# Selective scan with four states per partition group, its sums as 0/1 products one step later, and the gelu calls of a block kept together

## The chip, the cores and the metric

The kernel runs on one core of a Trainium2 chip. The core has five engines with a queue each, worked through in order: TensorE (PE, matrix products; its weight loads are listed apart as PEld), VectorE (DVE), ScalarE (ACT), GpSimd (POOL) and SyncE (SP, which here only issues transfers, DMAs). The time is the device time of one execution in microseconds (us). Of the kernel before, ten executions are known, and one more that the hardware profiler recorded.

## The reference, cut to what matters

The kernel computes four layers of a small sequence model on 8 sequences of 256 positions with 128 channels. The change touches two of its steps. One is the state space step of layer 1 (256 inner channels, 16 states):

```
x_ssm = xc @ W_xproj
delta_raw = x_ssm[..., :1]
Bm = x_ssm[..., 1:1 + D_STATE]
Cm = x_ssm[..., 1 + D_STATE:]
delta = softplus(delta_raw * w_dt + b_dt)
A = -exp(A_log)
dA = exp(delta[..., None] * A)
dBx = delta[..., None] * Bm[:, :, None, :] * xc[..., None]
h = dA_t * h + dBx_t                       # for each position t
y = einsum('bdn,bn->bd', h, c_t)
y = (y + xc * D_param) * silu(z)
```

The other is the feed-forward part of the local attention of layer 0, run twice for each sequence: `a, g = split(h @ w1 + b1)`, then `h = a * gelu(g)`, with 341 channels in `a` and in `g`.

## The kernel before

The kernel is a row of stages. The change lies in the stage `local_mamba` (function `local_mamba`, L818), which works on the 8 sequences one by one. Each sequence first goes through two layers of `local_block` (L666: local attention and the gated feed-forward, called "local work" below), and its result `x_local` goes to `mamba_sequence` (L713), the state space step. `interleave` (L249) weaves these generators into one program: up to four sequences in local work, up to two in the state space step. Each `yield` gives the weight after which that generator's turn comes again. The program order made so is a priority. A planner that models durations then fixes, when the kernel is built, the order in which each engine gets its instructions. On the chip every engine takes them in that order and waits on semaphores where an input is late. `issue_after` (L396) adds an order without a wait, `wait_for` (L406) a wait. A tile of a pool has a tag and a number of buffers (`bufs`); a new tile of that tag has to wait until the oldest is released.

In `mamba_sequence` the 256 inner channels lie as two groups of 128 on the partitions (index `c`). POOL works out `d` (delta) and `u` (delta times xc) in L770 to L774; DVE does it for the last sequence. The 33 rows of `x_ssm` are written to DRAM (L746) and read back, each row spread over all 128 partitions, by `rows` (L748): two DMAs of 256 KB for every pair of states, three buffers. The loop over 8 steps `m` (L778) takes two states for all 256 channels at a time. A step is four Exp on ACT (L785, 128 partitions by 255) into one of three tiles `da`, then three DVE instructions over 1024 columns: `u` times B (L787), the scan (L789), times C (L790), and last two products on PE with the identity (L792, 128 by 512 columns, fp32). These add the step to `yp`, one PSUM bank with a column for each position of each of the two channel groups. After the loop DVE reads `yp` in L796.

In `local_block`, three products `g` (L691, two of 128 output channels and one of 85) are followed by three Gelu on ACT (L693). Gelu and Silu need other function tables than Exp and Ln, so a table load stands at each change; `exp_ln` (L414) asks for the Exp and Ln table again after the last of the three.

At the end of the stage, `beside` (L904) runs next to the last sequence: weights for the next stages are loaded by SP, folded on PE, and the routing of the next layer starts (`route1`).

Of the kernel before, what the change touches and what calls it, by code (L numbers as in the profile page):

```python
# [21 lines left out]
P = 128  # L22
B = 8
S = 256
# [53 lines left out]
def _tables():  # L78
    f = np.float32
    cols, n = [], 0  # L80
# [45 lines left out]
    add("iota8", np.tile(np.arange(8, dtype=f) - 8, (P, 1)))  # L126
    _C["n"] = n
# [27 lines left out]
def _layout(d):  # L155
# [3 lines left out]
    out = {}  # L159
# [25 lines left out]
    put("alog", d["L1_attn_A_log"].reshape(2, P, 16).transpose(0, 2, 1))  # L185
# [111 lines left out]
class _Kernel:  # L297
    def __init__(self, ctx, tc, ins, out):
# [33 lines left out]
        r = slice(_C["iota32"][0], _C["n"])  # L332
        self.rt = const.tile([P, r.stop - r.start], F32, name="route_tables")
# [59 lines left out]
    def mm(self, out, lhsT, rhs, start=True, stop=True):  # L393
        return self.nc.tensor.matmul(out, lhsT, rhs, start=start, stop=stop)  # L394
# [271 lines left out]
    def local_block(self, l, x, w, rot, work, local, small, pools):  # L666
# [23 lines left out]
        for c in range(3):  # L690
            self.mm(part(c), w1[:, 341 + c * P : 341 + c * P + size(c)], h2)  # L691
        for c in range(3):
            last = nc.scalar.activation(ge[0 : size(c), c, :], part(c), AF.Gelu, bias=self.v(f"b1g{l}", c)[0 : size(c), :])  # L693
# [19 lines left out]
    def mamba_sequence(self, b, x, y, na, das, work, scan):  # L713
# [29 lines left out]
        xs = work.tile([33, S], F32, tag="xs", name="xs", bufs=2)  # L743
# [4 lines left out]
        def rows(m):  # L748

            bc = scan.tile([P, 2, 2, S], F32, tag="bc", name="bc", bufs=3)  # L750
            for k in range(2):
                r = 1 + 16 * k + 2 * m
                src = xd[r : r + 2, :].rearrange("n s -> (n s)").unsqueeze(0).to_broadcast([P, 2 * S])
                nc.sync.dma_start(bc[:, k].rearrange("p n s -> p (n s)"), src)
            return bc

# [4 lines left out]
        e, r, d, t = tile("e"), tile("r"), tile("d", 2), tile("t")  # L761
# [11 lines left out]
        u = tile("u", 2)  # L773
        eng.tensor_mul(u, d, xc)  # L774
        yield 3.0
        yp = self.psum("Y", "y")
        shp = [P, 2, 2, S]
        for m in range(8):  # L778
            bc = rows(m)
            bn, cn = (bc[:, k].unsqueeze(2).to_broadcast(shp) for k in range(2))  # L780
            da = das[m % len(das)]
            for n in range(2):
                for c in range(2):
                    i = 16 * c + 2 * m + n
                    nc.scalar.activation(da[:, n, c, 1:S], d[:, c, 1:S], AF.Exp, scale=na[:, i : i + 1])  # L785
            hs = scan.tile(shp, F32, tag="hs", name="hs", bufs=3)
            nc.vector.tensor_tensor(hs, u.unsqueeze(1).to_broadcast(shp), bn, ALU.mult)  # L787
            line = lambda a: a.rearrange("p n c s -> p (n c s)")
            nc.vector.tensor_tensor_scan(line(hs), line(da), line(hs), 0.0, ALU.mult, ALU.add)  # L789
            nc.vector.tensor_tensor(hs, hs, cn, ALU.mult)  # L790
            for n in range(2):
                self.mm(yp, self.ident, flat(hs[:, n]), m == 0 and n == 0, m == 7 and n == 1)  # L792
            yield 2.3
        yg = tile("t")
        for c in range(2):
            nc.vector.scalar_tensor_tensor(yg[:, c, :], xc[:, c, :], self.v("dpar", c), yp[:, c * S : (c + 1) * S], ALU.mult, ALU.add)  # L796
# [21 lines left out]
    def local_mamba(self):  # L818
        nc, tc = self.nc, self.tc
        w = self.w0  # L820
        with (
# [20 lines left out]
            for i in range(3):  # L842
                d = one.tile([P, 2, 2, S], F32, name=f"da{i}")
                nc.gpsimd.memset(d[:, :, :, 0:1], 0.0)
                das.append(d)
# [17 lines left out]
            tiles.append(scan.tile([P, 4, S], F32, tag="bc", name="rg", bufs=3))  # L863
# [949 lines left out]
```

## Time and profile before

| what | value |
|---|---|
| median of 10 executions | 1848.66 us (1846.89 to 1854.51) |
| profiled execution, its own time | 1847.66 us |
| its span, first to last instruction | 1845.9 us |
| mean granted TensorE clock | 0.927 |
| busy over the whole span | PE 84%, DVE 59%, ACT 56%, POOL 31% |
| stage `local_mamba` | about 40 us to 925 us after the start |
| scans of the eight sequences | 280 us to 903 us |

The page's busy shares are means over stages with different limits, so the stage is read from stretches of the span. The waits name who ended an engine's idle time. The chain of waits is followed back from the last instruction and says whose work stood in the way at each moment.

### The profile page before, as it was taken

How to read it: one execution, taken by the hardware profiler on the slowest of the kernel's cores; microseconds unless marked ns; L12 is line 12 of the kernel's file. 1: busy time of each engine (PE TensorE's matmuls, PEld its weight loads, DVE VectorE, ACT ScalarE, POOL GpSimd, SP SyncE). 2: the span in 40 equal slices, each digit the busy share in tenths (PEclk: the TensorE clock that was granted, in tenths of full speed). 3: DMA queues.
4: the chain of work that ended last, by engine and by line, in shares of the span. 5: the costliest groups of instructions: out<-in, count | busy, mean ns of one | idle time of the engine just before them, and what ended most of it. 6: DMA issues, size and time to landing. Idle time of an engine off the chain costs nothing.

```text
span 1845.9 us, 28438 instructions
## 1 busy us (share of the span) xinstructions
PE 1556.3 (84%) x10810; PEld 940.1 (51%) x10810; DVE 1095.5 (59%) x2016; ACT 1027.8 (56%) x2704; POOL 563.6 (31%) x493
## 2 busy tenths in 40 slices
PE   3677887878787867678669999999997999899997
PEld 2244553544454444344256766666663654465554
DVE  5725457777777776868724445557444223567664
ACT  4557777776777785556225454455443223465654
POOL 1314443433443323210421111110112025354552
PEclk7789998989999988887779999999998999899998
DMA  4000012010202111246440000000101311000000
GB/s 177 1 1 1 1 36 57 26 53 20 76 17 71 51 45 49 57 149 195 125 120 9 4 10 7 7 5 2 40 3 31 83 48 30 1 4 7 4 4 10
DMA packets 58329, 75.51 MB, mean 41 GB/s; under 512 B 5868, under 2 KB 35236, under 8 KB 57168
## 3 DMA queue, kind: packets, MB, share of 16 engines
q1 hardware_dynamic: 52864, 67.57, 12.9%
q0 software_dynamic: 3216, 5.07, 1.0%
q8 instruction: 85, 1.39, 0.3%
q10 hardware_dynamic: 2112, 1.05, 0.2%
q14 instruction: 52, 0.43, 0.1%
HBM read 65.46 MB, written 9.71 MB: 41 GB/s over the span
## 4 chain that ended last, share of the span: by engine, by line
PE 53%; DVE 19%; ACT 12%; issue 7%; POOL 6%; DMA 2%; POOLq 0%; DVEq 0%; SPq 0%; ACTq 0%
PE vps L394 7%; PE sc L394 7%; PE kps L394 6%; DVE hs L789 4%; PE out L394 4%; PE pt L475 4%; PE o L394 3%; PE pu L394 3%; ACT e L647 3%; PE pg L394 3%; DVE hs L790 3%; DVE hs L787 2%; PE acc L394 2%; PE y L394 2%; PE hps L394 2%
## 5 line engine op out<-in xcount | busy, mean ns | idle before, releaser
L394 PE MATMUL y<-hs,ident 128*128 128x512 f32 x256 | 143.9, 690 | 43.6 <-DVE hs L790 43.6
L789 DVE TENSOR_TENSOR_SCAN hs<-da,hs 128x1024 f32<-128x1024 f32 x64 | 148.7, 2332 | 4.0 <-ACT da L785 3.5
L475 PE MATMUL pt<-ident,e 128*128 128x128 f32 x768 | 123.7, 287 | 29.6 <-POOL e L652 19.8
L1682 ACT ACTIVATE e<-sc,nm 128x128 f32<-128x128 f32 (+1 forms) x256 | 104.1, 424 | 60.4 <-DVE nm L1677 60.0
L652 POOL TENSOR_TENSOR e<-e,rc 128x1024 f32<-128x1024 f32 x32 | 72.1, 2253 | 201.2 <-DVE rc L651 201.1
L785 ACT ACTIVATE da<-d,na 128x255 f32<-128x255 f32 x256 | 112.1, 502 | 34.9 <-DVE hs L789 17.4
L1685 POOL TENSOR_TENSOR e<-e,rc 128x1024 f32<-128x1024 f32 x48 | 91.9, 1915 | 127.7 <-DVE rc L1684 94.6
L647 ACT ACTIVATE e<-sc,nm,rn 128x128 f32<-128x128 f32 x256 | 113.4, 465 | 25.2 <-DVE nm L642 25.0
L475 PEld LDWEIGHTS pt<-ident,e 128*128 128x128 f32 x768 | 89.4, 145 | 72.3 <-POOL e L652 26.4
L599 POOL TENSOR_TENSOR t<-t,t 128x512 f32<-128x512 f32 x64 | 89.0, 1390 | 95.4 <-DVE t L586 86.4
L1294 POOL TENSOR_TENSOR e<-e,rc 128x512 f32<-128x512 f32 x32 | 33.6, 1051 | 273.2 <-DVE rc L1293 160.4
L787 DVE TENSOR_TENSOR hs<-u,bc 128x1024 f32<-128x1024 f32 x64 | 86.6, 1362 | 41.8 <-POOL u L774 26.5
L394 PEld LDWEIGHTS y<-hs,ident 128*128 128x128 f32 x256 | 50.3, 212 | 96.8 <-DVE hs L790 55.8
L1269 ACT COPY kp<-kps 128x512 f32<-128x512 f32 x128 | 74.8, 584 | 40.7 <-PE kps L394 40.2
L477 ACT COPY ptsb<-pt 128x512 f32<-128x512 f32 x89 | 52.2, 587 | 80.3 <-PE pt L475 78.5
L1118 POOL DMA_INDIRECT got<-ybuf,get x48 | 45.6, 950 | 154.2 <-DMA ybuf<-ys 113.2
L477 DVE COPY ptsb<-pt 128x512 f32<-128x512 f32 x103 | 69.1, 685 | 32.0 <-PE pt L475 31.6
L394 PE MATMUL qk<-w_local,h 128*128 128x512 f32 x128 | 72.6, 655 | 17.8 <-DVE t L586 13.0
L790 DVE TENSOR_TENSOR hs<-hs,bc 128x1024 f32<-128x1024 f32 x64 | 82.0, 1289 | 0.2
L1677 DVE TENSOR_REDUCE nm<-sc 128x4 f32<-128x1024 f32 (+1 forms) x48 | 58.6, 1221 | 25.4 <-PE sc L394 25.1
L394 PE MATMUL sc<-km,q 64*128 64x512 f32 x192 | 70.5, 655 | 1.7 <-DVE FunctionType.Silu _12235 L1500 0.9
L1242 DVE BATCH_NORM_STATS2 st<-out 128x6 f32<-128x128 f32 x80 | 20.0, 288 | 81.0 <-PE out L394 74.0
(394 smaller groups left out, 3845.4 us busy)
## 6 DMA issues: line engine op xcount, KB each, us to landing
bc<-xs SPq DMA_DIRECT2D x128, 256.0 KB, 4.5
w_attn<-in_w_dram SPq DMA_DIRECT2D x4, 1024.0 KB
w_local<-in_w_dram SPq DMA_DIRECT2D x2, 1557.0 KB
places<-zeros SPq DMA_DIRECT2D x2, 1280.0 KB
w_moe<-in_e1gate_dram SPq DMA_DIRECT2D x8, 256.0 KB
w_moe<-in_e1up_dram SPq DMA_DIRECT2D x8, 256.0 KB, 7.7
w_moe<-in_e1down_dram SPq DMA_DIRECT2D x8, 256.0 KB, 5.4
w_moe<-in_e2rg_dram SPq DMA_DIRECT2D x8, 256.0 KB
```

Of the source, the lines that this page charges most:

```text
L394: return self.nc.tensor.matmul(out, lhsT, rhs, start=start, stop=stop)
L475: self.last = self.nc.tensor.transpose(pt[:, j * P : (j + 1) * P], src[:, j * P : (j + 1) * P], self.ident)
L477: self.nc.any.tensor_copy(sb.rearrange("p a b -> p (a b)"), pt)
L599: nc.gpsimd.tensor_add(t1, t1, t2)
L647: nc.scalar.activation(e[:, j, g, :], scs[:, j, g, :], AF.Exp, bias=nm[:, j, g : g + 1], scale=rq[:, j, g : g + 1], accum_out=sm[:, j, g : ...
L785: nc.scalar.activation(da[:, n, c, 1:S], d[:, c, 1:S], AF.Exp, scale=na[:, i : i + 1])
L787: nc.vector.tensor_tensor(hs, u.unsqueeze(1).to_broadcast(shp), bn, ALU.mult)
L789: nc.vector.tensor_tensor_scan(line(hs), line(da), line(hs), 0.0, ALU.mult, ALU.add)
L790: nc.vector.tensor_tensor(hs, hs, cn, ALU.mult)
L1269: nc.scalar.copy(k[:, 2 * i : 2 * i + 2, :].rearrange("p a b -> p (a b)"), ps)
L1682: nc.scalar.activation(e[:, i, :], sc[:, i, :], AF.Exp, bias=nm[:, i : i + 1], accum_out=sm[:, i : i + 1])
L1685: nc.gpsimd.tensor_tensor(e, e, rc.unsqueeze(2).to_broadcast([P, n, keys]), ALU.mult)
```

## The change

There are two parts.

**State space step.** A step now takes four states of 32 channels on the 128 partitions (partition 32n + h is state n of channel h) and four such groups of 32 channels along the columns, so the eight steps are two channel halves `c` by four sets `m` of four states. DVE and ACT run the same number of instructions of the same size. What feeds them changes: `d` and `u` are written to DRAM (`put`), and for each half `c` read back four times, once for each quarter of the partitions (`copies`, four DMAs for `d` and four for `u`; `d` has one buffer, `u` two). The second half is fetched after the first product of step 3. B and C of all 16 states come in one tile `bc` with one buffer, by four DMAs at the start of the sequence. The sum over the four states is a product with a 0/1 table `sum4` of 128 by 32: four products of 32 output channels by 256 columns for each step, each on its own quarter of the PSUM partitions. The sums of a step are put into the program one step later and ordered behind the PE instruction that was last put into the program before them. The scan steps of a sequence begin in the program only when those of the sequence before are all in it (`self.scanned`). `xs` has one buffer in place of two, `d` one, `u` takes over the buffer of `r`, and a step yields 2.5 in place of 2.3.

**Gelu.** The three Gelu of a block get high priority in the planner, and the first of them waits for the third product `g`.

```diff
+    add("sum4", i % 32 == np.arange(32)[None])
...
-    put("alog", d["L1_attn_A_log"].reshape(2, P, 16).transpose(0, 2, 1))
+    put("alog", d["L1_attn_A_log"].reshape(8, 32, 4, 4).transpose(2, 0, 3, 1))
...
-            self.mm(part(c), w1[:, 341 + c * P : 341 + c * P + size(c)], h2)
-        for c in range(3):
-            last = nc.scalar.activation(ge[0 : size(c), c, :], part(c), AF.Gelu, bias=self.v(f"b1g{l}", c)[0 : size(c), :])
+            m = self.mm(part(c), w1[:, 341 + c * P : 341 + c * P + size(c)], h2)
+        with self.tc.high_priority():
+            for c in range(3):
+                last = nc.scalar.activation(ge[0 : size(c), c, :], part(c), AF.Gelu, bias=self.v(f"b1g{l}", c)[0 : size(c), :])
+                if c == 0:
+                    self.wait_for(last, m)
...
-        def rows(m):
-            bc = scan.tile([P, 2, 2, S], F32, tag="bc", name="bc", bufs=3)
-            for k in range(2):
-                r = 1 + 16 * k + 2 * m
-                src = xd[r : r + 2, :].rearrange("n s -> (n s)").unsqueeze(0).to_broadcast([P, 2 * S])
-                nc.sync.dma_start(bc[:, k].rearrange("p n s -> p (n s)"), src)
-            return bc
+        bc = scan.tile([P, 2, 4, S], F32, tag="bc", name="bc", bufs=1)
+        for n in range(4):
+            src = bass.AP(tensor=xd.tensor, offset=xd.offset + (1 + n) * S, ap=[[0, 32], [4 * S, 8], [1, S]])
+            nc.sync.dma_start(bc[32 * n : 32 * n + 32].rearrange("p k m s -> p (k m) s"), src)
...
+        dram = [self.dram.tile([2 * P, S], F32, name=f"{n}{b}") for n in "du"]
+        def put(k, a):
+            nc.sync.dma_start(dram[k].rearrange("(c p) s -> p c s", c=2), a)
+        def copies(k, c):
+            a = scan.tile([P, 4, S], F32, tag="du"[k], name="du"[k], bufs=1 + k)
+            for n in range(4):
+                nc.sync.dma_start(a[32 * n : 32 * n + 32], dram[k][c * P : (c + 1) * P, :].rearrange("(g h) s -> h g s", h=32))
+            return a
...
-        u = tile("u", 2)
+        put(0, d)
+        u = tile("r")
         eng.tensor_mul(u, d, xc)
+        put(1, u)
+        dr, ur = copies(0, 0), copies(1, 0)
         yield 3.0
+        while self.scanned < b:
+            yield 0.5
         yp = self.psum("Y", "y")
-        shp = [P, 2, 2, S]
-        for m in range(8):
-            bc = rows(m)
-            bn, cn = (bc[:, k].unsqueeze(2).to_broadcast(shp) for k in range(2))
-            da = das[m % len(das)]
-            for n in range(2):
-                for c in range(2):
-                    i = 16 * c + 2 * m + n
-                    nc.scalar.activation(da[:, n, c, 1:S], d[:, c, 1:S], AF.Exp, scale=na[:, i : i + 1])
+        summed = deque()
+        def add(i, hs, last):
+            c, m = i // 4, i % 4
+            for g in range(4):
+                j = self.mm(yp[32 * g : 32 * g + 32, c * S : (c + 1) * S], self.c("sum4"), hs[:, g, :], m == 0, m == 3)
+                self.issue_after([j], last)
+        shp = [P, 4, S]
+        for i in range(8):
+            c, m = i // 4, i % 4
+            da = das[i % len(das)]
+            for g in range(4):
+                nc.scalar.activation(da[:, g, 1:S], dr[:, g, 1:S], AF.Exp, scale=na[:, 8 * m + 4 * c + g : 8 * m + 4 * c + g + 1])
             hs = scan.tile(shp, F32, tag="hs", name="hs", bufs=3)
-            nc.vector.tensor_tensor(hs, u.unsqueeze(1).to_broadcast(shp), bn, ALU.mult)
+            nc.vector.tensor_tensor(hs, ur, bc[:, 0, m, :].unsqueeze(1).to_broadcast(shp), ALU.mult)
+            if i == 3:
+                dr, ur = copies(0, 1), copies(1, 1)
             nc.vector.tensor_tensor_scan(line(hs), line(da), line(hs), 0.0, ALU.mult, ALU.add)
-            nc.vector.tensor_tensor(hs, hs, cn, ALU.mult)
-            for n in range(2):
-                self.mm(yp, self.ident, flat(hs[:, n]), m == 0 and n == 0, m == 7 and n == 1)
-            yield 2.3
+            nc.vector.tensor_tensor(hs, hs, bc[:, 1, m, :].unsqueeze(1).to_broadcast(shp), ALU.mult)
+            summed.append((i, hs))
+            last = self.pe_last
+            if i:
+                add(*summed.popleft(), last)
+            yield 2.5
+        add(*summed.popleft(), self.pe_last)
+        self.scanned = b + 1
```

More of the change, by code (lines that the diff above doesn't have):

```diff
@@ L332, in __init__ @@
         r = slice(_C["iota32"][0], _C["n"])
+        self.scanned = 0
         self.rt = const.tile([P, r.stop - r.start], F32, name="route_tables")
@@ L393, in mm @@
     def mm(self, out, lhsT, rhs, start=True, stop=True):
-        return self.nc.tensor.matmul(out, lhsT, rhs, start=start, stop=stop)
+        self.pe_last = self.nc.tensor.matmul(out, lhsT, rhs, start=start, stop=stop)
+        return self.pe_last
     def issue_after(self, later, earlier):
@@ L742, in mamba_sequence @@
             self.mm(ps[0:33, 0:S], wx[:, c, :], xc[:, c, :], c == 0, c == 1)
-        xs = work.tile([33, S], F32, tag="xs", name="xs", bufs=2)
+        xs = work.tile([33, S], F32, tag="xs", name="xs", bufs=1)
         nc.scalar.copy(xs, ps[0:33, 0:S])
@@ L759, in mamba_sequence @@
         yield 1.0
-        e, r, d, t = tile("e"), tile("r"), tile("d", 2), tile("t")
+        e, r, d, t = tile("e"), tile("r"), tile("d"), tile("t")
+        dram = [self.dram.tile([2 * P, S], F32, name=f"{n}{b}") for n in "du"]
[6 more added lines that the diff above has]
+            return a
         for c in range(2):
@@ new lines, in add @@
+        def add(i, hs, last):
[4 more added lines that the diff above has]
+        shp = [P, 4, S]
+        line = lambda a: a.rearrange("p g s -> p (g s)")
+        for i in range(8):
[3 more added lines that the diff above has]
+                nc.scalar.activation(da[:, g, 1:S], dr[:, g, 1:S], AF.Exp, scale=na[:, 8 * m + 4 * c + g : 8 * m + 4 * c + g + 1])
@@ L786, in mamba_sequence @@
             hs = scan.tile(shp, F32, tag="hs", name="hs", bufs=3)
-            nc.vector.tensor_tensor(hs, u.unsqueeze(1).to_broadcast(shp), bn, ALU.mult)
-            line = lambda a: a.rearrange("p n c s -> p (n c s)")
+            nc.vector.tensor_tensor(hs, ur, bc[:, 0, m, :].unsqueeze(1).to_broadcast(shp), ALU.mult)
+            if i == 3:
+                dr, ur = copies(0, 1), copies(1, 1)
             nc.vector.tensor_tensor_scan(line(hs), line(da), line(hs), 0.0, ALU.mult, ALU.add)
-            nc.vector.tensor_tensor(hs, hs, cn, ALU.mult)
@@ L842, in local_mamba @@
             for i in range(3):
-                d = one.tile([P, 2, 2, S], F32, name=f"da{i}")
-                nc.gpsimd.memset(d[:, :, :, 0:1], 0.0)
+                d = one.tile([P, 4, S], F32, name=f"da{i}")
+                nc.gpsimd.memset(d[:, :, 0:1], 0.0)
                 das.append(d)
@@ L862, in local_mamba @@
             tiles = [scan.tile([P, 4, S], F32, tag="hs", name="rg", bufs=3) for _ in range(3)]
-            tiles.append(scan.tile([P, 4, S], F32, tag="bc", name="rg", bufs=3))
+            tiles.append(scan.tile([P, 4, S], F32, tag="d", name="rg", bufs=1))
             def one_sequence(b):
```

## The prediction

> **What bounds the kernel now.** I read the page's busy times first, then stretches of the stage, the finish of each sequence's local work, the chain, the waits, and the rows that price each edit. Over the whole span PE is the fullest engine:
>
> ```profile
> PE 1556.3 (84%) x10810; PEld 940.1 (51%) x10810; DVE 1095.5 (59%) x2016; ACT 1027.8 (56%) x2704; POOL 563.6 (31%) x493
> ```
>
> That is a mean over stages the change doesn't touch. In the changed stage (columns: length, busy us of PE, PEld, DVE, ACT, POOL with instruction counts, granted clock, DMA share, GB/s):
>
> ```profile
> 231.00:277.00 46.00, 38.38 (x282) 23.03 (x280) 26.56 (x51) 34.15 (x98) 19.19 (x22) 1.00 0.12 36
> 507.00:554.00 47.00, 40.18 (x276) 24.23 (x274) 37.02 (x52) 35.23 (x96) 22.73 (x22) 1.00 0.08 17
> 738.00:784.00 46.00, 29.51 (x129) 16.31 (x130) 39.43 (x36) 27.04 (x75) 13.69 (x2) 0.81 0.23 58
> ...
> 264.00:840.00 576.00, 443.45 (x2286) 254.57 (x2286) 436.98 (x514) 405.83 (x993) 201.79 (x168) 0.92 0.22 60
> 840.00:925.00 85.00, 57.02 (x229) 30.48 (x227) 61.87 (x94) 35.06 (x73) 25.62 (x18) 0.74 0.56 154
> ```
>
> Before the scans join (231 to 277) PE is busy 83%; with them 85%. It looks like PE's ceiling here. But from 264 to 840 PE, DVE and ACT are full to 77%, 76% and 70%: no engine is alone. The local work hands over its results at these times:
>
> ```profile
> 240.97 0.42 DVE L441 TENSOR_TENSOR x_local<-ln,ln_rs 128x256 f32<-128x256 f32 x1 [1.37 <-ACT ln_rs L440]
> ...
> 783.23 0.41 DVE L441 TENSOR_TENSOR x_local<-ln,ln_rs 128x256 f32<-128x256 f32 x1
> ...
> 839.18 0.39 DVE L441 TENSOR_TENSOR x_local<-ln,ln_rs 128x256 f32<-128x256 f32 x1
> ```
>
> So local work ends at 839, and only the last sequence's state space step follows: its scans run from 864 to 903, eight steps of some 5 us, back to back on DVE. A gain must bring 839 forward; what lengthens the last state space step adds in full. The sums `y` in the two stretches, then the chain from 264 to 840 and its waits:
>
> ```profile
> 264.00:840.00 576.00, 117.35 (x216) 41.34 (x216) 5.51 (x12) 0.92 0.22 60
> 840.00:925.00 85.00, 26.55 (x40) 8.99 (x40) 1.82 (x4) 0.74 0.56 154
> ```
>
> ```profile
> by line: DVE hs L789 11.4%; issue 11.2%; DVE hs L790 6.8%; DVE hs L787 6.1%; PE y L394 4.7%; ACT e L647 4.6%; DVE nm L641 3.2%; POOL e L652 3.0%; DMA bc<-xs 2.2%; POOL t L601 1.9%; DVE ge L701 1.6%; PE pt L475 1.6%; PE w L394 1.6%; POOL e L
> ```
>
> ```profile
> DVE hs L787 <- POOL u L774: 26.5, 7, 6.4
> DVE hs L787 <- DMA bc<-xs: 13.6, 6, 3.8
> ...
> ACT da L785 <- POOL d L772: 16.5, 7, 3.7
> ...
> PE y L394 <- DVE hs L790: 29.9, 23, 3.5
> ```
>
> PE spends 117.35 us, a quarter of its work there, on sums, and stands 29.9 us in 23 waits because a sum came up in its queue before DVE had finished the step. On the chain the three DVE scan lines hold 24.3%, the sums 4.7%. The rows that price the edits:
>
> ```profile
> 263.72 0.38 SPq L746 DMA_DIRECT2D xs<-xs  x1
> 265.18 2.94 SPq L754 DMA_DIRECT2D bc<-xs  x6
> ...
> 331.26 1.09 PE L394 MATMUL o<-ptsb,v 128*64 128x128 f32 x16
> 332.29 1.12 PE L394 MATMUL y<-hs,ident 128*128 128x512 f32 x2
> ...
> 365.38 0.60 PE L604 MATMUL qkt<-ident,t 128*128 128x128 f32 x4
> 365.82 1.02 PE L394 MATMUL qk<-w_local,h 128*128 128x512 f32 x2
> ```
>
> ```profile
> L693 ACT ACT_TABLE_LOAD x22 | 28.2, 1283 | 0.3
> ```
>
> ```profile
> bc<-xs SPq DMA_DIRECT2D x128, 256.0 KB, 4.5
> ```
>
> **Part by part.** What stays: 64 steps of four Exp and three DVE instructions, same sizes; POOL's four operations for each sequence. DVE's 317 us (148.7 + 86.6 + 82.0) are not reduced.
>
> *A, the sums.* Columns streamed stay 1024 a step, as four products of 256 instead of two of 512; all that can be saved is their running side by side. The nearest row is `o`, which alternates between two halves of the output partitions: 16 instructions start to next start in 1.03 us, 0.064 each, where full-width products of the same 128 columns take 0.44/4 = 0.11. That is 1.71 times. Serial tiles give 1, four truly parallel ones 4. I take 1.71, because each fp32 product is two instructions here (256 for 128), and the second needs the same tile as the first. Then 117.35 becomes 68.6 and 48.7 us go. One step (5 us of DVE) later exceeds the longest wait, 3.5, so I let all 29.9 go. PE is freed of at most 78.6 us. What reaches 839? At least the sums' own part of the chain, 4.7% of 576 = 27 us, times 0.415 = 11. At most what DVE leaves: its fullest stretch is 39.43/46 = 86%, and 437/0.86 = 508, so 68. PE near its ceiling in stretches such as 507 to 554 speaks for the upper end, DVE's equal mean filling for the lower. I take a little over the middle: -44.
>
> Here the Trainium skill speaks on both sides. The trace shows the change from half-width `o` to full-width `y` at 332.29 with no gap of its own to see. "TensorEngine Tiling (Array Packing)", section Tiling Modes, says that changing the tiling mode drains the engine, which would speak against 64 such changes; it gives no price, so the sum by the row keeps -44. "TensorE: Matmul & The Clock Gate", section Part 3, lists 2.38 times for three column tiles; as an estimate by that page 117.35 becomes 49, and A would be about -54.
>
> *B, the clock.* Where PE did 38 to 40 us in 46 it was granted 1.00; at 29.51, 0.81. A less busy PE gets less. PE keeps 443 - 49 = 394 us; 0 to 4% more is 0 to 16. I take +6.
>
> *C, gelu.* 16 blocks need 16 loads; there are 22, and each of the 6 extra ones brings one back: 12 x 1.283 = 15.4 us of ACT at most. The new wait for the third `g` holds ACT's queue (everything behind it: Exp of attention and scan, copies) by up to two products, 0.86 us, 16 times: +14 at most. ACT is not the fullest; I take -4.
>
> *D, the round trip of d and u, sequences 0 to 6.* Transfers go from 17 to 23 a sequence (1 + 4 + 2 + 16) and from 4 MB to 3.5 MB, in 1 KB pieces instead of 2 KB. SP issues them in about 0.45 us each, 10 us in a period of some 90, so its queue has room. But it waits in order: `put` of `d` for POOL, the copies for the puts, and `bc` for the last L790 of the sequence before (long done at today's spacing). Before, L787 needed only `u`. Now: the 33 KB write and its read are 1.46 us apart, so a 256 KB put is about 3; eight copies issue in 3.6 us and land 3.5 to 4.5 later. That puts `ur` 9 us after `u`. Behind the waiting L787 stand all of DVE's local reductions, and behind the waiting Exp all of ACT; both then hold PE. Bounds: nothing if the planner puts local work ahead (and the 13.6 us of `bc` waits go, as all rows come early), or 7 x 9 = 63. Waits of this kind reached the chain nearly whole (2.2% of 576 = 12.7 of 13.6 us). The planner was 2.3 us too hopeful for each late `bc`; with two transfers in series I take 4.6 x 7 = 32, less 13.6: +18. The fetch of the second half waits for the Exps of step 3 (`d` has one buffer); they run up to three `da` tiles, 15 us of DVE, ahead of the scan, which covers 7; uncovered it costs up to 7 more each. In the tail the weight loads of the next stage stand behind these waits on SP, up to 3 us, with 24 us until the first use after the stage.
>
> *E, the last sequence.* Nothing covers its 9 us. Its final sum shrinks from 3.78 us to about 2.5 at the low clock (`wout`, half the columns at one width, takes 2.08). +8; bounds +3 to +12.
>
> Sum: -44 + 6 - 4 + 18 + 8 = -16 us on the profiled execution's 1847.66 (span 1845.9, 1.8 around it). The median is 1.0 higher: 1848.66 - 16 = 1833.
>
> **Rivals.**
> 1. *Slower: the round trip is exposed.* At every sequence start L787 and the first Exp stand in front of DVE's and ACT's queues for the full 9 us. D becomes 63 - 13.6 = +49, the sum +15: 1864. For it: 7 of 7 starts already wait for POOL's `u`, 3.8 us each, so the planner is hopeful there. Against: it does model transfers, and `bc` was late only 6 times in 64 steps. It decides from 6.8 us exposed a start (D = +34).
> 2. *Much faster: DVE becomes the bound.* A = -68, B = 0, C = -8, D = 0, E = +8: -68, 1781. For it: PE at 83 to 85% with and without scans. Against: DVE must hold 86% throughout.
> 3. *PE was not the limit.* The chain is DVE's and latencies'; only A = -11 arrives, with B = +2: +13, 1862. For it: 24.3% against 4.7%.
> 4. *The change doesn't do what it says:* the four tiles run one after another; sums keep 117 us, and of the waits half arrives: A = -15, B = +2: +9, 1858. Against: `o` does overlap.
>
> **How the numbers follow.** Forecast 0.42 (its own range 1815 to 1845), rival 1 0.18, rival 2 0.20, rival 3 0.12, rival 4 0.08. What a measurement of this kernel can tell from no change is about 0.2%, 3.7 us. Faster: the forecast and rival 2 less 0.02 at the forecast's edge, 0.60; within 0.2%: that edge and the near edges of rivals 3 and 4, 0.06; slower 0.34. The range of 8 in 10 runs from 1785 (little of rival 2 lies below) to 1868 (rivals 1 and 3 with a worse draw lie above).
>
> **What would show it.** A: PE's sums in the stage near 70 us outside the tail, waits of `y` for L790 nearly gone, the eighth `x_local` about 35 us earlier than 839. Sums above 110 us: rival 4; near 35: four tiles in parallel. B: a granted clock under 0.92. C: 16 table loads at the gelu line, and PE `g` named as releaser of its waits. D: waits of L787 and of the Exps for DMA in place of POOL, about 4.6 us a start; 7 and more is rival 1. E: 70 us or more from the last `x_local` to the last scan, now 64. The planner's whole order shifts with such a change, and an unlucky order of local work is what would make this wrong without any one of these lines showing why.

## The result, and the profile after

The changed kernel takes 1928.57 us (median of 8), the kernel before 1848.23 (median of 28 by now): ratio 1.0429, 95% interval 1.0418 to 1.0440. The forecast was 1833 with a range of 1785 to 1868. It was wrong in sign and by 96 us. The profiled execution of the changed kernel took 1922.96 us (span 1921.2).

First the busy times, then the stretches of the stage (columns as before: length, busy us of PE, PEld, DVE, ACT, POOL, granted clock, DMA share, GB/s):

```profile
PE 1529.7 (80%) x11066; PEld 923.6 (48%) x11066; DVE 1095.9 (57%) x2007; ACT 1018.9 (53%) x2699; POOL 549.1 (29%) x493
```

```profile
264.00:840.00 576.00, 404.84 (x2406) 229.13 (x2408) 403.90 (x478) 373.73 (x945) 186.16 (x164) 0.81 0.17 39
840.00:925.00 85.00, 46.30 (x259) 26.65 (x260) 49.34 (x55) 40.53 (x83) 8.19 (x8) 0.71 0.58 160
925.00:1005.00 80.00, 28.28 (x161) 15.05 (x161) 52.11 (x77) 21.78 (x48) 23.42 (x19) 0.54 0.38 93
```

From 264 to 840 *every* engine did less than before: PE 405 us (443), DVE 404 (437), ACT 374 (406). DVE's work over the whole kernel is unchanged (1095.9 against 1095.5), so what is missing was not saved but put off: the stage now runs on into 925 to 1005. The same stretches for the sums `y` alone:

```profile
264.00:840.00 576.00, 43.55 (x380) 9.02 (x383) 4.34 (x10) 0.81 0.17 39
840.00:925.00 85.00, 8.36 (x72) 1.63 (x72) 1.75 (x4) 0.71 0.58 160
925.00:1005.00 80.00, 8.65 (x64) 1.60 (x64) 0.87 (x2) 0.54 0.38 93
```

The sums fell to 60.6 us in all, from 143.9. So the products do what they were meant to do, and the time rose all the same. When the local work hands over its first, seventh and eighth sequence:

```profile
249.34 0.42 DVE L446 TENSOR_TENSOR x_local<-ln,ln_rs 128x256 f32<-128x256 f32 x1 [1.98 <-ACT ln_rs L445]
...
800.54 0.42 DVE L446 TENSOR_TENSOR x_local<-ln,ln_rs 128x256 f32<-128x256 f32 x1 [0.22 <-ACT ln_rs L445]
...
867.03 0.42 DVE L446 TENSOR_TENSOR x_local<-ln,ln_rs 128x256 f32<-128x256 f32 x1 [2.83 <-ACT ln_rs L445]
```

The eighth comes at 867 instead of 839, and the last scan ends at 983.7 instead of 904.0: 79.7 us later. That is the whole difference: the two profiled executions differ by 75.3 us, since behind the stage the changed kernel is some 4 us shorter. Of the 79.7 us, 27.9 lie ahead of the eighth `x_local` and 51.8 behind it. The chain from 264 to 840:

```profile
by line: DVE hs L818 14.4%; issue 8.9%; DVE hs L815 7.2%; DVE hs L819 5.5%; ACT e L652 5.2%; PE pt L480 3.3%; PE qk L398 3.0%; PE ln L398 2.6%; PE sc L398 2.6%; ACT L700 2.0%; ACT ge L700 1.9%; ACT da L813 1.9%; PE o L398 1.9%; PE wo L398 1
```

The waits over the whole execution (line, releaser: us, times, longest), then the two rows for the sums of the kernel before, over the whole execution, and of the changed kernel from 264 to 840:

```profile
PEld y L398 <- DVE hs L819: 139.7, 37, 17.6
PE y L398 <- DVE hs L819: 112.4, 24, 17.4
...
ACT da L813 <- DVE hs L818: 27.0, 12, 5.0
ACT da L813 <- DMA d<-d: 25.7, 5, 6.9
...
DVE hs L815 <- DMA u<-u: 9.0, 1, 9.0
```

```profile
PE y L394 <- DVE hs L790: 43.6, 29, 3.8
```

```profile
PE y L398 <- DVE hs L819: 48.6, 16, 6.7
```

The sums are no longer among the first lines of the chain, and DVE's three scan lines have grown on it, 24.3% to 27.1%. So have other products of PE: `pt` from 1.6% to 3.3%, and `qk`, `ln` and `sc`, which were not among the first lines before, hold 2.6 to 3.0% each. PE stands 112.4 us in front of the sums in the whole execution, where before it stood 43.6; from 264 to 840 it is 48.6 for 29.9, and most of the growth lies behind 840. This wait catches the eye, and the runs below show that it is not the cause.

**One chain of eight scans.** In both kernels the `xs` of a sequence (its B, C and step size, written to DRAM) goes out only when the scan of the sequence before has ended or nearly so: on PE `xps` comes behind the other sequence's `wout`, but for sequence 4 of the changed kernel. This is the order that the planner made, and no hard rule (e13 below breaks it). So from the first `xs` to the last scan product the time is one row of pieces: *start* (`xs` to the first product `hs<-u,bc`), *scan* (to the last product `hs<-hs,bc`), *gap* (to the next `xs`). In us, from the start times in the timeline:

| sequence | 0 | 1 | 2 | 3 | 4 | 5 | 6 | 7 | sum |
|---|---|---|---|---|---|---|---|---|---|
| start, before | 10.6 | 12.3 | 14.2 | 11.8 | 11.3 | 12.2 | 10.7 | 10.3 | 93.5 |
| start, after | 34.3 | 32.8 | 34.1 | 38.1 | 41.9 | 29.5 | 27.8 | 29.8 | 268.4 |
| scan, before | 62.8 | 58.9 | 57.0 | 58.7 | 62.9 | 49.4 | 39.2 | 39.9 | 428.8 |
| scan, after | 52.2 | 57.4 | 55.0 | 53.6 | 48.2 | 39.0 | 37.3 | 35.7 | 378.4 |
| gap behind, before | 24.8 | 24.1 | 20.2 | 17.9 | 14.2 | 8.9 | 7.8 | | 118.0 |
| gap behind, after | 19.4 | 13.3 | 13.0 | -0.2 | 6.4 | 7.5 | 5.7 | | 65.1 |

The first `xs` is 8.2 us later (271.9 for 263.7). Then +174.9 of starts, -50.4 of scans, -52.9 of gaps: +79.8, the whole loss. This table adds up by its making; what causes what, only the experiments can say. From sequence 4 on the gaps are 6 to 8 us and the last scans 36 to 39 (eight steps back to back on DVE), so that little is left there to give way to a late start.

What a start consists of, in the timeline of the changed kernel (start, length, engine, instruction):

```profile
583.35 0.31 SPq L755 DMA_DIRECT2D xs<-xs  x1
...
591.87 1.26 POOL L789 TENSOR_TENSOR d<-d,r 128x512 f32<-128x512 f32 x1
593.16 0.38 SPq L771 DMA_DIRECT2D d<-d  x1
593.21 1.26 POOL L792 TENSOR_TENSOR r<-d,xc 128x512 f32<-128x512 f32 x1
594.50 0.38 SPq L771 DMA_DIRECT2D u<-r  x1
595.30 1.76 SPq L776 DMA_DIRECT2D d<-d  x4
597.16 3.69 SPq L776 DMA_DIRECT2D u<-u  x8
...
603.39 1.28 ACT L700 ACT_TABLE_LOAD   x1
...
614.61 3.29 ACT L813 ACTIVATE da<-d,na 128x255 f32<-128x255 f32 x8
...
617.85 1.23 DVE L646 TENSOR_REDUCE nm<-sc 128x8 f32<-128x1024 f32 x1 [2.89 <-PE sc L398]
...
621.49 2.35 DVE L815 TENSOR_TENSOR hs<-u,bc 128x1024 f32<-128x1024 f32 x2
```

The page's list of transfers of the changed kernel (count, size, median us from issue to landing):

```profile
d<-d SPq DMA_DIRECT2D x64, 128.0 KB, 2.8
u<-u SPq DMA_DIRECT2D x64, 128.0 KB, 3.5
```

`u` is ready 11 us after `xs`, as before. The last copy of its first half is issued near 599 and lands 3.5 us later, near 602.5: the trip takes 8 us. But the first Exp comes at 614.6 and the first product at 621.5. These further 19 us are no wait for a DMA: local instructions stand ahead in the queues of ACT and DVE (37 ACT instructions between this sequence's `d<-e` and its first Exp, 5 in the kernel before). ACT works through them up to the first Exp; four table loads of 1.28 us are among them. DVE is idle for some 14 of the 19 us, because the local instructions ahead of the first product wait for PE and ACT, as `nm<-sc` does.

### The profile page after: what moved, and what is told of

Same layout as the page of the kernel before. It is cut to its first block, busy times and chain, and to the rows that moved or that the text cites. A ratio compares the mean times of both kernels' runs of the same rounds, so it can differ in the third digit from the quotient of the medians.

```text
span 1921.2 us, 28974 instructions
## 1 busy us (share of the span) xinstructions
PE 1529.7 (80%) x11066; PEld 923.6 (48%) x11066; DVE 1095.9 (57%) x2007; ACT 1018.9 (53%) x2699; POOL 549.1 (29%) x493
## 4 chain that ended last, share of the span: by engine, by line
PE 56%; DVE 18%; ACT 12%; issue 7%; POOL 4%; DMA 2%; SPq 0%; POOLq 0%; DVEq 0%; ACTq 0%
PE vps L398 7%; PE sc L398 7%; PE kps L398 5%; DVE hs L818 5%; PE pt L480 4%; PE out L398 4%; PE o L398 3%; PE pu L398 3%; PE pg L398 3%; ACT e L652 3%; DVE hs L815 2%; PE ln L398 2%; DVE hs L819 2%; PE acc L398 2%; PE qk L398 2%
## 5 line engine op out<-in xcount | busy, mean ns | idle before, releaser
L480 PE MATMUL pt<-ident,e 128*128 128x128 f32 x768 | 133.7, 303 | 37.3 <-POOL e L657 17.3
L818 DVE TENSOR_TENSOR_SCAN hs<-da,hs 128x1024 f32<-128x1024 f32 x64 | 154.2, 2431 | 1.5 <-ACT da L813 1.5
L398 PE MATMUL y<-hs,route_tables 128*32 128x256 f32 x512 | 60.6, 536 | 113.0 <-DVE hs L819 112.4
L813 ACT ACTIVATE da<-d,na 128x255 f32<-128x255 f32 x256 | 107.7, 500 | 52.7 <-DVE hs L818 27.0
L480 PEld LDWEIGHTS pt<-ident,e 128*128 128x128 f32 x768 | 94.9, 153 | 84.2 <-issue 28.0
L1715 ACT ACTIVATE e<-sc,nm 128x128 f32<-128x128 f32 (+1 forms) x256 | 104.0, 424 | 59.1 <-DVE nm L1710 58.7
L1718 POOL TENSOR_TENSOR e<-e,rc 128x1024 f32<-128x1024 f32 x48 | 91.9, 1915 | 127.3 <-DVE rc L1717 94.3
L652 ACT ACTIVATE e<-sc,nm,rn 128x128 f32<-128x128 f32 x256 | 113.5, 463 | 14.5 <-DVE nm L647 14.2
L482 ACT COPY ptsb<-pt 128x512 f32<-128x512 f32 x98 | 57.4, 586 | 117.5 <-PE pt L480 115.8
L398 PE MATMUL qk<-w_local,h 128*128 128x512 f32 x128 | 80.1, 717 | 25.7 <-DVE t L591 19.3
L815 DVE TENSOR_TENSOR hs<-u,bc 128x1024 f32<-128x1024 f32 x64 | 87.1, 1384 | 9.1 <-DMA u<-u 9.0
L398 PE MATMUL sc<-msk,identb 128*128 128x512 bf16 (+2 forms) x224 | 54.4, 375 | 40.3 <-ACT e L652 40.2
L398 PEld LDWEIGHTS y<-hs,route_tables 128*32 128x32 f32 x512 | 12.3, 127 | 148.8 <-DVE hs L819 139.7
L482 DVE COPY ptsb<-pt 128x512 f32<-128x512 f32 x94 | 62.9, 685 | 31.8 <-PE pt L480 31.7
```

Of the source, the lines that this page charges most:

```text
L398: self.pe_last = self.nc.tensor.matmul(out, lhsT, rhs, start=start, stop=stop)
L480: self.last = self.nc.tensor.transpose(pt[:, j * P : (j + 1) * P], src[:, j * P : (j + 1) * P], self.ident)
L482: self.nc.any.tensor_copy(sb.rearrange("p a b -> p (a b)"), pt)
L652: nc.scalar.activation(e[:, j, g, :], scs[:, j, g, :], AF.Exp, bias=nm[:, j, g : g + 1], scale=rq[:, j, g : g + 1], accum_out=sm[:, j, g : ...
L813: nc.scalar.activation(da[:, g, 1:S], dr[:, g, 1:S], AF.Exp, scale=na[:, 8 * m + 4 * c + g : 8 * m + 4 * c + g + 1])
L815: nc.vector.tensor_tensor(hs, ur, bc[:, 0, m, :].unsqueeze(1).to_broadcast(shp), ALU.mult)
```

## The experiments

Short names: *starts* and *gaps* are the sums above. In the groups e1 to e4 and e12 to e14 the kernel before itself took 1903 to 1904 us on the chip in use, elsewhere 1847 to 1849; every ratio is against the kernel before on the same chip. The extra 55 us lie behind the stage (994 to 1001 us follow the last scan product in the traces of these groups, 936 to 948 in the others), so places within the stage are compared directly. The expectations of e1 to e4 are in us of the first chip; scaled by the ratio, e1 to e4 are 1853, 1911, 1908 and 1842 there.

| kernel | ratio, 95% interval | starts | gaps | scans | 8th `x_local` | last scan ends | PE `y` waits for DVE |
|---|---|---|---|---|---|---|---|
| before | 1 | 93.5 | 118.0 | 428.8 | 839.2 | 904.0 | 43.6 |
| changed | 1.0429 [1.0418, 1.0440] | 268.4 | 65.1 | 378.4 | 867.0 | 983.7 | 112.4 |
| e1 changed, reads the previous d, u | 1.0025 [1.0014, 1.0036] | 162.1 | 95.3 | 383.5 | 807.8 | 910.2 | 53.0 |
| e2 changed, sums at once | 1.0340 [1.0314, 1.0367] | 257.3 | 57.5 | 386.4 | 856.2 | 972.2 | 109.2 |
| e3 changed, gelu as before | 1.0326 [1.0302, 1.0351] | 263.4 | 63.2 | 377.1 | 853.1 | 969.0 | 106.2 |
| e4 before + gelu | 0.9968 [0.9951, 0.9985] | 96.5 | 126.7 | 410.0 | 834.7 | 900.6 | 40.9 |
| e5 before + 1 round trip | 1.0143 [1.0125, 1.0161] | 149.0 | 129.6 | 389.5 | 856.8 | 933.9 | 66.8 |
| e6 changed, early prologue | 1.0642 [1.0624, 1.0660] | 263.1 | 171.7 | 322.4 | 918.6 | 1030.2 | 136.8 |
| e7 before, early prologue | 1.0155 [1.0134, 1.0175] | 80.7 | 201.4 | 390.9 | 879.9 | 937.2 | 63.6 |
| e8 e1 + early prologue | 1.0456 [1.0436, 1.0476] | 187.7 | 192.2 | 340.4 | 922.3 | 990.6 | 109.6 |
| e9 changed, 2 of 8 sums | 1.0374 [1.0349, 1.0399] | 269.0 | 62.8 | 373.4 | 859.3 | 976.3 | 111.1 |
| e10 before, 2 of 16 sums | 0.9937 [0.9913, 0.9962] | 94.3 | 90.6 | 444.8 | 820.5 | 892.4 | 38.3 |
| e11 changed, wide copies | 1.0418 [1.0388, 1.0447] | 243.4 | 66.8 | 398.1 | 851.4 | 975.5 | 104.1 |
| e12 before + 2 round trips | 1.0174 [1.0153, 1.0196] | 189.6 | 110.2 | 377.0 | 829.1 | 939.2 | 79.2 |
| e13 changed, scan spread | 1.0393 [1.0376, 1.0411] | 309.2 | -2.8 | 402.8 | 873.7 | 979.5 | 67.7 |
| e14 before + gelu, scan spread | 1.0014 [1.0000, 1.0028] | 96.5 | 119.4 | 423.6 | 842.3 | 906.7 | 32.4 |
| e15 before + 3 round trips | 1.0488 [1.0467, 1.0508] | 252.3 | 124.3 | 352.3 | 865.7 | 994.8 | 97.1 |
| e16 e15 + gelu | 1.0520 [1.0490, 1.0551] | 250.0 | 133.9 | 345.9 | 877.9 | 1002.0 | 104.2 |
| e17 e11 + e2 + e3 | 1.0365 [1.0348, 1.0382] | 238.4 | 78.2 | 392.2 | 849.2 | 973.3 | 150.3 |

### Which part of the change costs it (e1 to e4)

**e1**, the copies take `d` and `u` of the sequence before, so nothing waits for the puts:

```diff
+        source = dram if b == 0 else self.before
+        self.before = dram
-                nc.sync.dma_start(a[32 * n : 32 * n + 32], dram[k][c * P : ...
+                nc.sync.dma_start(a[32 * n : 32 * n + 32], source[k][c * P : ...
```

> The kernel after, but the four-fold copies of d and u read what the sequence before wrote to DRAM (the first sequence reads its own), so they no longer wait for this sequence's writes; the writes stay, and the numbers of the state space step are those of the wrong sequence. Late-start theory (the round trip through DRAM sets the first scan product 28 to 42 us after the xs transfer, against 10 to 14 before, and the state space step falls behind the local work): the start comes back to 10 to 20 us for most sequences and the time falls from 1928 to 1870 or less. Sums theory (PE stands in front of sums that DVE has not finished, 112 us against 44): nothing about the sums changes, so 1915 to 1930. Gelu theory: 1920 to 1930.

75 of the 80 us are gone with every transfer still issued. Not the bytes, then, nor their number in SP's queue, but that the scan must wait for its own `d` and `u`. The layout, the sums, the buffers and the gelu part of the change are all in e1, and together they cost 0.25%. The local work even ends at 807.8, 31 us ahead of the kernel before, and the two whole scans still left at that point use the gain up (tail of 102.4 us for 64.8).

**e2**, the sums right behind their own step, with no issue order:

```diff
-                self.issue_after([j], last)
...
-            summed.append((i, hs))
-            last = self.pe_last
-            if i:
-                add(*summed.popleft(), last)
+            add(i, hs, None)
             yield 2.5
-        add(*summed.popleft(), self.pe_last)
```

> The kernel after, with the four products of a step put into the program right behind the step and with no issue order given. Sums theory: PE's waits for L819 fall from 112 us to 45 or less and the time by 40 us or more, to 1890 or less. Late-start theory: the start of the scans stays 28 us or more behind the xs transfer and the time stays within 15 us of 1928. Gelu theory: the same, 1928.

1.0340, a loss of 66 us in place of 80: putting the sums one step later, with their issue order, costs some 14 us here and gains nothing. The waits hardly fell (109.2 us), as the late-start theory said; the time, 1911, is 2 us below its band.

**e3**, the gelu part taken out of the changed kernel, and **e4**, the gelu part alone in the kernel before (the diff of the change, at `last = nc.scalar.activation(ge...)`):

```diff
-        with self.tc.high_priority():
-            for c in range(3):
-                last = nc.scalar.activation(ge[0 : size(c), c, :], ...)
-                if c == 0:
-                    self.wait_for(last, m)
+        for c in range(3):
+            last = nc.scalar.activation(ge[0 : size(c), c, :], ...)
```

> The kernel after, with the gelu part of before (no priority, no wait). Gelu theory (its priority and its wait push scan and attention work back on ACT): 1890 or less. Late-start and sums theories: 1915 to 1945, table loads at the gelu line up from 16 to some 22.

> The kernel before, with the gelu part of the change alone. Gelu theory: 30 us or more above before. Late-start and sums theories: within 12 us of 1848, with 16 table loads in place of 22 at the gelu line (up to 15 us of ACT less), rather below than above.

Alone the gelu part is a small gain, 0.32%; this version beats both kernels. In the changed kernel it is a loss of about 1% (1.0429 against 1.0326); e3's 1908 lies between the two bands that were forecast, so gelu carries a part of the loss, the smaller one. The table loads fell as predicted, here the group of the changed kernel (before: 22):

```profile
L700 ACT ACT_TABLE_LOAD x16 | 20.5, 1283 | 0.1
```

### A round trip in the kernel before (e5), and an earlier prologue (e6 to e8)

**e5**:

```diff
         eng.tensor_mul(u, d, xc)
+        for a, n in ((d, "d"), (u, "u")):
+            there = self.dram.tile([2 * P, S], F32, name=f"{n}{b}").rearrange("(c p) s -> p c s", c=2)
+            nc.sync.dma_start(there, a)
+            nc.sync.dma_start(a, there)
         yield 3.0
```

> The kernel before, in which d and u are written to DRAM and read back into their own tiles (two writes and two reads of 256 KB a sequence) ahead of the scan; nothing else of the change. Late-start theory: the first scan product comes 18 to 25 us after the xs transfer in place of 10 to 14, the sequences fall behind one another, and the kernel is 1.5 to 4% slower than before. If the late start is only harmful together with the rest of the change: within 0.5% of before.

One trip costs 1.4% on its own, just under the range: starts 55 us later in sum, 15 to 23 us each, 30 us later at the end.

**e6** (changed), **e7** (before), **e8** (e1): the four yields ahead of the scan a quarter as long, so that the prologue stands earlier in the program:

```diff
-        yield 2.0
+        yield 0.5
...
-        yield 1.0
+        yield 0.25
...
-        yield 3.0
+        yield 0.75
```

> The kernel after, with the four yields ahead of the scan (2, 2, 1, 3) shortened to a quarter (0.5, 0.5, 0.25, 0.75), so that a sequence's xs, d and u come earlier in the program order against local work; the transfers and their waits stay. Late-start theory: the start stays 25 us or more behind xs, but xs follows x_local by 10 to 20 us in place of 22 to 51, the stretch from the last x_local to the last scan shrinks from 117 to 90 us or less, and the ratio to before falls from 1.043 to 1.02 or less. If it is the sums or the clock that costs: 1.035 to 1.05.

> The kernel before with the same short yields ahead of the scan. If its state space step also lags behind the local work, 0.5 to 2% faster than before; if local work sets the pace alone, within 0.5%.

> The short yields together with copies that read what the sequence before wrote (the numbers of the state space step are those of the wrong sequence). Late-start theory: with both the lag and the wait gone the cheaper sums show, local work ends 30 us earlier as in the run with the copies of the sequence before, and the ratio to before is 0.985 or less. If the sums' saving is lost for another reason: 0.995 to 1.01.

The obvious cure makes it worse, in all three, and none of the outcomes forecast came. The starts change little (in e8 they grow), the gaps grow to 171.7, 201.4 and 192.2 us, and in e6 and e8 the first five scans run in bursts of 40 to 48 us. The local work comes late instead: its eighth result at 918.6, 879.9 and 922.3. In e7 the starts are shorter than in the kernel before (80.7 us) and the time is longer: short starts alone don't make the stage fast.

### Is it PE? (e9, e10)

**e9**, in `add` of the changed kernel; **e10**, in the kernel before:

```diff
             c, m = i // 4, i % 4
+            if m < 3:
+                return
             for g in range(4):
-                j = self.mm(yp[...], self.c("sum4"), hs[:, g, :], m == 0, m == 3)
+                j = self.mm(yp[...], self.c("sum4"), hs[:, g, :])
```

```diff
-            for n in range(2):
-                self.mm(yp, self.ident, flat(hs[:, n]), m == 0 and n == 0, m == 7 and n == 1)
+            if m in (3, 7):
+                self.mm(yp, self.ident, flat(hs[:, 1]), m == 3, m == 7)
```

> The changed kernel with the sums of steps 3 and 7 alone on PE (8 instead of 32 products a sequence); the sums of the other six steps are left out of the computation. DVE and ACT keep all their steps and the same order, and the late start of each scan stays. If PE's standing in front of the sums is what costs the time (112 us of waits in the changed kernel, with local work queued behind them), those waits fall under 50 us, the granted clock of the stage goes back from 0.80 to 0.85 or more, and the time comes back to 0.99 to 1.01 of the kernel before. If the late start alone costs it, through the order on ACT and DVE and the tail, the sums hardly matter: 1.025 to 1.04, last scan product still at 965 or later.

> The kernel before with one product (the second half) of steps 3 and 7 alone on PE, 2 of 16 a sequence; the other sums are left out of the computation. This bounds term A of the prediction from outside: about 126 of 144 us of PE's sums and most of the 43.6 us of waits go, and nothing else changes. The prediction gave 44 us for 79 us freed; if that share holds here, 160 us freed must give 80 us or more (0.957 or less). If PE is not the limit (rival 3, the chain is DVE's), 10 to 25 us: 0.986 to 0.995.

Stretches of e10, whole and for its sums:

```profile
264.00:840.00 576.00, 408.20 (x2153) 247.44 (x2151) 444.21 (x524) 396.97 (x990) 198.56 (x168) 0.82 0.24 67
```

```profile
264.00:840.00 576.00, 24.05 (x28) 6.17 (x28) 6.39 (x14) 0.82 0.24 67
```

The sums from 264 to 840 went from 117 to 24 us and the kernel gained 0.63%, 11.6 us; DVE does 444 us there for 437. PE stands idle 168 of the 576 us in place of 133, and the time hardly moves: that PE was full was not the limit. But the clock took back a part of what was freed. PE's other work took 326 us for 2070 products before (443.45 less 117.35) and 384 us for 2125 here (408.20 less 24.05), 15% longer each, at a granted clock of 0.82 for 0.92. As an estimate, some 49 of the 93 us came back in this way. So the run shows that the lower clock does not outweigh the work left out, not that it is free. In e9 PE still stands 111 us, now in front of ten sums:

```profile
PE y L398 <- DVE hs L821: 111.1, 10, 27.0
```

My expectation that the waits would fall under 50 us failed; the time, 1.0374, lies where the late start alone was to put it (1.025 to 1.04). It is 11 us less loss than in the changed kernel, about what the sums left out gave in e10. PE stands there because DVE's scan is late, whatever is to be summed. e13 (67.7 us of waits, 1.0393) and e17 (150.3 us, 1.0365) say the same: the wait does not carry the time.

### Fewer transfers, other spacing (e11, e13, e14)

**e11**: each half of `d` and `u` is put by itself in the order in which it is read, and comes back in one transfer over 128 partitions (code shortened):

```diff
-            nc.sync.dma_start(dram[k].rearrange("(c p) s -> p c s", c=2), a)
+            for c in range(2):
+                there = bass.AP(tensor=dram[k].tensor, offset=dram[k].offset + c * P * S, ap=[[S, 4], [4 * S, 32], [1, S]])
+                nc.sync.dma_start(there, a[:, c, :])
...
-            for n in range(4):
-                nc.sync.dma_start(a[32 * n : 32 * n + 32], ...)
+            src = bass.AP(tensor=there.tensor, offset=there.offset + c * P * S, ap=[[0, 4], [4 * S, 32], [1, 4 * S]])
+            nc.sync.dma_start(a.rearrange("p g s -> p (g s)"), src)
```

> The changed kernel with the round trip in fewer, wider transfers: d and u are put half by half, so that a half lies in the order in which it is read, and each half comes back in one transfer over all 128 partitions instead of four over 32: 8 transfers a sequence instead of 18, the same bytes. If the late start is what starts the trouble, the scans begin some 5 to 10 us earlier after xs (25 to 32 us instead of 28 to 42) and a part of the loss comes back: 1.015 to 1.035, PE's waits at the sums between 75 and 105 us. If the start does not matter, 1.04 to 1.045.

Starts 25 us less in sum, ratio the same within its interval: a miss, and the ratio lies where "the start does not matter" was to put it. So the sum of the starts does not set the time by itself. Here the one wide transfer is late and its waits are exposed, 107 us in the whole execution against 34.7, and the scans are 20 us longer in sum:

```profile
DVE hs L818 <- DMA u<-u: 60.1, 8, 14.8
...
ACT da L816 <- DMA d<-d: 46.7, 9, 12.0
```

The longest of these waits, in the timeline: the second of the two `u` copies follows the first at 684.72, and the product is released by the first, 12.7 us after its issue.

```profile
682.89 2.33 SPq L779 DMA_DIRECT2D u<-u  x2
...
695.65 3.50 DVE L818 TENSOR_TENSOR hs<-u,bc 128x1024 f32<-128x1024 f32 x3 [14.77 <-DMA u<-u]
```

**e13** yields 2.8 for 2.5 at each step of the changed kernel; **e14** adds the gelu part to the kernel before and yields 2.7 for 2.3:

```diff
-            yield 2.5
+            yield 2.8
```

> The changed kernel with 2.8 in place of 2.5 yielded for a step, so that in the program the steps of a scan stand among more of the local work. If dense scans and the stretches without one cost the time, the scans of the first five sequences lengthen from 48 to 57 us to 55 us and more, the stretches without a scan shrink from 333 us to under 310, and the ratio is 1.02 to 1.037. If the late start costs it in itself, however the steps lie, 1.04 or more.

> The kernel before with the gelu part of the change (alone 0.9968) and 2.7 in place of 2.3 yielded for a step. By the same theory the scans lengthen, the 211 to 223 us without a scan shrink to under 200, and the time falls to 0.985 to 0.993. If the spacing of the steps does not matter, 0.995 to 1.000; a tail that grows with the later scans could make it 1.000 to 1.010.

In e13 the scans lengthen by 24 us, the starts by 41, and the gaps vanish (-2.8 us for all seven: the last `xs` goes out 16 us before the scan ahead of it ends). The stretches without a scan shrink from 333 to 306 us, as hoped, and the last scan ends only 4 us earlier: what the gaps gave, starts and scans took. The ratio, 1.0393, lies between the two forecasts. In e14 the spacing loses what gelu had gained. Both expectations that spread scans would be worth something failed.

### Does the late start suffice? (e12, e15 to e17)

**e12**, **e15**: e5 with two and with three trips (`for i in range(2)`, `range(3)`, around the four lines); **e16**: e15 with the gelu part; **e17**: e11 with e2 and e3.

```diff
         for a, n in ((d, "d"), (u, "u")):
+            for i in range(3):
```

> The kernel before, with d and u each sent to DRAM and back twice in place; sums, steps and layout as before. One such round trip made the start of the eight scans later by 55 us in sum (93.5 to 149.0 us from xs to the first scan product) and the time 1.0143. If it is the stretches without a scan under way that cost the time, each us of them about half a us, two round trips bring the starts to some 200 to 240 us in sum, the stretches without a scan from 211 us to 300 to 340 us, and the time to 1.025 to 1.04, as slow as the changed kernel with none of its sums or layout. If the four-state layout or the sums on PE carry the loss of the changed kernel, the second trip costs no more than the first: 1.015 to 1.028.

> The kernel before with three round trips of d and u in place of two. One gave starts of 149 us in sum, 30 us later an end of the scans and 1.0143; two gave 189.6 us, 35 us and 1.0174. A third should bring the starts to 230 to 250 us, close to the changed kernel's 268. If the late start carries the changed kernel's loss, by then all slack is used up and the last scan product comes at 960 to 980 in place of 904, ratio 1.03 to 1.042. If it goes on as from one trip to two, some 5 to 10 us more for 40 us of start, 1.019 to 1.024, and more than half of the changed kernel's loss must lie elsewhere.

> The same with the gelu part of the change added. Alone it gave 0.9968 in the kernel before; in the changed kernel taking it out gave 1.0326 in place of 1.0429, so there it costs 1%. If it costs where the scans start late, this is 0.5 to 1.2% slower than three round trips alone; if its cost belongs to the changed kernel's own order, 0.3% faster to the same.

> The changed kernel with three parts mended together: one wide transfer for each half of d and u, gelu as before the change, and the sums put in right behind their own step. Each alone gave 1.0418, 1.0326 and 1.034 where the changed kernel has 1.0429. If their gains add, 1.020 to 1.026; if they are the same slack counted three times, 1.03 to 1.035. Still above 1, since the starts stay above 200 us in sum.

e15 is the kernel before, with its layout, its sums and its gelu, and starts of 252 us: 1.0488, more than the changed kernel. Its waits, over the whole execution, and its stretch:

```profile
PE y L394 <- DVE hs L795: 97.1, 30, 28.6
...
DVE hs L792 <- DMA u<-u: 33.2, 6, 16.3
...
ACT da L790 <- DMA d<-d: 20.1, 4, 16.6
```

```profile
264.00:840.00 576.00, 428.89 (x2178) 244.57 (x2177) 391.48 (x476) 383.45 (x944) 181.68 (x163) 0.89 0.26 78
```

With sums that nobody touched, PE's waits for them went from 43.6 to 97.1 us, and DVE does 391 us in the stretch for 437. So the marks of the changed kernel, standing PE and an emptier DVE, come with the round trips alone. As there, the waits for DMA (53 us) are far smaller than the growth of the starts (159 us).

The dose is not even: starts of 149, 190 and 252 us give 1.0143, 1.0174 and 1.0488. With two trips the local work still ended early (829.1) and all was lost behind it; with three both moved. e12's expectation missed, e15's upper bound too. e16 against e15 doesn't tell whether gelu costs where scans start late (the intervals overlap). In e17 the three mended parts do not add: 1.0365, above both forecasts, where e3 alone has 1.0326. Why it is no better than e3 is not shown.

## Why the prediction was wrong, step by step

Two steps failed: A, the worth of PE's time, and above all D, the price of the round trip. As an estimate, some 32 of the 96 us lie in A (44 forecast, 11.6 in e10). The rest is what the late start cost in D and E, with whatever B and C cost inside the changed kernel, which no run separates.

- **A, the sums (-44): a failed step.** Its engine part was too modest: one step's sums take 0.64 us where they took 1.88, 2.9 times faster, not the 1.71 of `o`. (Before, then after, timeline of PE, both at a granted clock of 1.00; over the whole execution, with more of it at a lower clock, 143.9 us became 60.6, 2.4 times. The full-width `xin` follows the quarter-width products without a gap.)

```profile
340.68 1.88 PE L394 MATMUL y<-hs,ident 128*128 128x512 f32 x4
```

```profile
341.97 0.64 PE L398 MATMUL y<-hs,route_tables 128*32 128x256 f32 x8
342.54 1.13 PE L398 MATMUL xin<-x_local,w 128*128 128x256 f32 x4
```

  The Trainium skill's page "TensorE: Matmul & The Clock Gate", Part 3, with 2.38 times for three tiles, was nearer than the row I chose. What failed is what a saved us of PE is worth. I read PE's 83 to 85% as a ceiling and took 44 of 79 us; e10 frees 93 us of sums in the stage and gains 11.6. That is rival 3, "PE was not the limit", which put A at -11. That "all 29.9" of the waits would go was wrong in kind: a wait in front of a sum shows how late DVE is, and from 264 to 840 it rose to 48.6, in the whole execution from 43.6 to 112.4.
- **B, the clock (+6, at most 16).** It fell further than I allowed, 0.92 to 0.81. PE's other work from 264 to 840 took 361 us for 2026 products, where 326 us did 2070 before: 13% longer each, some 42 us of PE. How much of that reached the end is not shown. It does not explain the loss: e10 is faster than the kernel before at 0.82, and e15 loses 4.9% at 0.89.
- **C, gelu (-4).** 16 loads, and alone -0.32%, 5.9 us: right. That the same edit costs 1% inside the changed kernel was not foreseen, and its mechanism stays open.
- **D, the round trip (+18): the failed step that set the result.** The trip itself was well sized (9 us forecast, 8 seen). The waits for DMA of Exp and L815, by which I priced it, are even smaller than forecast: 14.3 us up to 925, where 32 stood in the sum for sequences 0 to 6, and 20.4 more in the last sequence. The error was to price it by these waits. The starts are 22 us later each, not 4.6 or 9, because other work is put ahead of the first Exp and the first product, and then no engine is seen to wait for the DMA. Rival 1 had the sign and its place but the same price list, and at most 63 us. The unit to count in was the chain of eight state space steps: +175 us of starts against 103 us of gaps and longer scans that could give way.
- **E, the last sequence (+8, at most 12).** The stretch behind the eighth `x_local` grew by 51.8 us. I took it that only one state space step follows the local work. After the change, the scan of sequence 6 begins at 875, later than the eighth `x_local` at 867, so two whole scans and a start are left. And SP's queue, which I expected to hold up weight loads, held up the copies: in the last sequence they stood behind a load that waited 12.7 us for its buffer (SP's timeline).

```profile
925.37 0.38 SPq L771 DMA_DIRECT2D u<-r  x1
938.51 0.37 SPq L1164 DMA_DIRECT2D w_moe<-in_e1gate_dram x1
938.93 0.53 SPq L1164 DMA_DIRECT2D w_moe<-in_e1up_dram x1
939.55 1.92 SPq L776 DMA_DIRECT2D d<-d  x4
```

  The wait of that queue, from 900 to 950:

```profile
SPq L1164 <- PE less L398: 12.7, 1, 12.7
```

- **Last sentence.** "An unlucky order of local work" does carry part of it: of the 22 us that a start grew by, some 8 are the trip and the rest is order. But it is not luck: the starts grew in every kernel here whose scan waits for data sent out and read back. Why the order puts 15 to 40 ACT instructions ahead of the first Exp, rather than the 8 us of work that the trip needs, wasn't settled; in e1, where only the dependence is gone, the starts are still 162 us, 69 more than in the kernel before, at a loss of 0.25%.

## What to carry to other kernels

Find first what is strictly in series from one end of the stage to the other, and count a change in that chain: how often its delay is passed, how much slack each link has, and from which link on there is none. High shares of busy time and waits in front of an engine's instructions did not show it here; a table of start, work and gap for each link did. An engine at 85% need not be the limit: leave a part of its work out and see what the time does, which costs a few lines. Read the granted clock with it, since in e10 about half of PE's freed time came back as longer products.

## What the runs showed of the hardware that I had not expected

- Four products of 32 output channels by 256 columns, on four quarters of the output partitions, ran 2.9 times as fast as two of 128 channels by 512 (0.64 against 1.88 us a step), and no gap shows at the change between the widths.
- With 93 us of PE's work left out in a stretch of 576 us (e10) the granted clock fell from 0.92 to 0.82, and PE's other products took 15% longer each. PE's busy share does not give the clock by itself: in e5 PE is busy 444 us of the 576, as in the kernel before, at 0.89.
- One transfer of 512 KB that writes each row to four quarters of the partitions released DVE 12.7 us after its issue and left it waiting up to 14.8 us (e11); four of 128 KB to a quarter each landed 2.8 to 3.5 us after issue.
